# Whole PSUM banks in a kernel's plan, and layer 1's scores tied to layer 0's column products

## Chip, cores and metric

The kernel runs on one core of a Trainium2 chip. The metric is the device time of one launch in microseconds. The kernel before takes 2768.54 us (median of three runs, 2766.03 to 2769.21).

## What is computed

Sixty-four graphs, each with 256 nodes of 256 features (`x`) and a 256 x 256 adjacency (`adj`), go through four layers; each adds to its input and normalizes, all in float32. Cut to what matters (`lrelu` has slope 0.01, `ln` normalizes rows):

```python
# layer 0, 4 heads of 64
X, q, k = heads(lrelu(x @ W_lin + b)), heads(lrelu(x @ W_q)), heads(lrelu(x @ W_k))
adj_h = adj[:, None] * sigmoid(q @ k.T / 8)
deg = sum(adj_h, axis=-1); dis = where(deg > 0, deg ** -0.5, 0)
x = ln(x + ln(dis[..., :, None] * adj_h * dis[..., None, :] @ X) * g + b)
# layer 1, 8 heads of 32
s = where(adj > 0, heads(x @ Wq + bq) @ heads(x @ Wk + bk).T / sqrt(32), NEG)
x = ln(x + softmax(s) @ heads(x @ Wv + bv) @ Wo + bo)
# layer 2
h = (eps * x + adj @ x) @ W1 + b1                      # 1024 wide
x = ln(x + silu(rmsnorm(h) * w) @ W2 + b2)
# layer 3, one head
Wh = x @ W; e = leaky_relu(Wh @ a1 + (Wh @ a2).T, 0.2)
x = ln(x + gelu(ln(softmax(where(adj > 0, e, NEG)) @ Wh) * gamma + beta))
```

## The kernel before

A graph is two blocks of 128 rows by 256 columns, and nearly every operation handles one graph whole: 128 partitions by 2 x 256 numbers. `graph` (L250) lists all operations of one graph; it runs for 64 graphs. It does not issue them. Each call of `op` records the engine, a cost in ns written by hand, the function that issues the instructions, and which `Value`s (tiles) are written and read. `Plan.order` (L98) then puts the some 17,000 operations of all graphs in one order, and `emit` (L737) issues them in that order; each engine works off its own instructions in it, and semaphores are set by the framework from what each tile is written and read by.

The order is that of a list scheduler. It keeps a clock for each engine. Again and again it takes, of all operations whose inputs are planned, the one that can start first, at a tie the one due first. `AHEAD` (L31) limits how early a load may be planned: only when its due turn is at most so many turns away. A turn is a use of one ScalarE table: sigmoid, exp, SiLU and gelu follow each other, four turns to a round, and `ROUND` (L35) says that a graph does layer 0 in its first round, layer 1 two rounds later, layer 2 after five and layer 3 after seven. So in one round some eight graphs at different layers share the engines. `SLOTS` (L37) says how many tiles of each kind there are: the kind "p" is PSUM, eight banks of 512 numbers each in a partition. A tile takes a slot when it is first written and gives it back after its last use.

Most PSUM tiles hold two halves (2 x 256). `Value(..., parts)` lets the plan keep track of parts: a tuple such as `(ps, o)` in the list of writes or reads means this half alone, so that a reader of one half and the writer of the other don't depend on each other in the plan.

TensorE works in three kinds of operation, which the plan calls modes: full (128 x 128 weights; transposes count as a fourth, "transpose"), rows (products with 32 or 64 rows of contraction, placed side by side: L444, layer 0's scores, and L524, layer 1's scores, in two operations of four heads each), and columns (results of 32 or 64 partitions side by side: L462, layer 0's degrees; L484, layer 0's attention times values; L560, layer 1's attention times values). The table `CHANGE` (L23) holds what the plan takes for a change between modes, and `STAY` (L32) a penalty that keeps it from leaving a tiled mode.

Names that come up: L320 is a product of weights with a transposed input, L331 one with the transposed input as weights, L275 a transpose, L591 layer 2's adjacency product, L603 its first and L645 its second dense product, L608 and L610 the two ScalarE reads of L603's result (square, and scale with bias), L622 and L631 the mean of squares and its broadcast with GpSimd's power L626 in between, L635 the multiplication and L637 the SiLU. L407 is the masked softmax's VectorE pass over one half of a bank of scores, L412 its exponential on ScalarE. L660 and L669 belong to layer 3. All DMAs are issued by SyncE (SP), among them the loads (L267) and transposes through device memory (L287 to L306, L547, L549).

Of the kernel before, what the change touches and what calls it, by code (L numbers as in the profile page):

```python
# [19 lines left out]
PE_MM, PE_TR = 432, 109  # L20
# [7 lines left out]
DMA_KB, DMA_SEEN = 4, 1900  # L28

WORDS = {"s": 516, "d": 1024, "b": 2048, "c": 32, "p": 512, "h": 1024}  # L30
AHEAD = 14  # L31
STAY = 200  # L32
NEAR = 1, 1, 3

ROUND = 0, 2, 5, 7  # L35
TAIL = 0, 2, 3, 4
# [42 lines left out]
class Plan:  # L79
# [6 lines left out]
        self.ops, self.turns = [], {}  # L86
        self.graph = 0

    def op(self, engine, cost, fn, w=(), r=(), turn=None, mode="full", after=None, size=0):
        pair = lambda x: x if isinstance(x, tuple) else (x, None)  # L90
        w, r = [pair(x) for x in w], [pair(x) for x in r]
        op = Op(engine, cost, fn, w, r, self.graph, turn, mode, after, size)
        op.table = turn is not None and engine == "ACT"
        if op.table:
            self.turns[turn] = self.turns.get(turn, 0) + 1
        self.ops.append(op)

    def order(self):  # L98
        for i, op in enumerate(self.ops):
            op.index = i  # L100
        for op in reversed(self.ops):
            op.due = min((nxt.due for nxt in op.after), default=4 * (min(op.graph + ROUND[3], self.graphs - 1 + TAIL[3]) + 1))
            if op.turn is not None:
                op.due = min(op.due, op.turn)
        clock = {e: 0.0 for e in AFTER}
        self.free = {k: [(0.0, i) for i in range(n)] for k, n in SLOTS.items()}
        turns, left = sorted(self.turns), dict(self.turns)
        turn, loaded, mode, moved = 0, None, "full", 0.0
        ready = {op for op in self.ops if not op.waits}
        done = []  # L110
        self.busy = {e: 0.0 for e in AFTER}
        while ready:
            best = None
            for op in ready:
                if (op.due - AHEAD if op.first else op.turn or 0) > turns[turn]:
                    continue
                start = clock[op.engine]
                if op.engine == "PE" and mode in ("rows", "columns") and mode != op.mode:
                    start += STAY - 60 * (op.mode == "transpose")
                start = max(start, op.ready)  # L120
                need = {}
                for v in op.values:
                    if v.slot is None:
                        need[v.kind] = need.get(v.kind, 0) + 1
                for kind, n in need.items():
                    free = self.free[kind]
                    if len(free) < n:
                        break
                    start = max(start, sorted(free)[n - 1][0])
                else:  # L130
                    key = start, op.due, op.graph, op.index
                    if best is None or key < best[0]:
                        best = key, start, op
            if best is None:
                raise RuntimeError(f"the plan is stuck at {len(done)} of {len(self.ops)}")
            _, start, op = best
            op.start = start
            ready.discard(op)
            if op.table and op.turn != loaded:
                op.start, loaded = op.start + TABLE_LOAD, op.turn  # L140
            if op.engine == "PE":
                op.start = max(op.start, clock["PE"] + CHANGE.get((mode, op.mode), 0))
                mode = op.mode
            end = clock[op.engine] = op.start + op.cost
            op.landed = end + op.seen
            if op.engine == "SP":
                moved = max(moved, end) + op.size * DMA_KB
                op.landed = max(op.landed, moved + DMA_SEEN)
            self.busy[op.engine] += op.cost
            done.append(op)  # L150
            op.takes = [v for v in op.values if v.slot is None]
            for v in op.takes:
                self.free[v.kind].sort()
                v.slot = self.free[v.kind].pop(0)[1]
            for v in op.values:
                v.uses -= 1
                v.end = max(v.end, op.landed)
                if not v.uses:
                    self.free[v.kind].append((v.end, v.slot))
            for nxt in op.after:  # L160
                nxt.waits -= 1
                nxt.ready = max(nxt.ready, end + ITSELF[op.engine] if nxt.engine == op.engine != "SP" else op.landed)
                if not nxt.waits:
                    ready.add(nxt)
            if op.table:
                left[op.turn] -= 1
                while turn < len(turns) - 1 and not left[turns[turn]]:
                    turn += 1
        assert len(done) == len(self.ops)
        self.span = max(op.start + op.cost for op in done)  # L170
        return sorted(done, key=lambda op: op.start)
# [78 lines left out]
def graph(plan, nc, c, t, out, b):  # L250

    op = plan.op
# [6 lines left out]
    SIG, EXP, SILU, GELU = range(4)  # L259

    def turn(layer, func):
        return 4 * min(b + ROUND[layer], plan.graphs - 1 + TAIL[layer]) + func
# [159 lines left out]
    xT, adjT, x, adj = load("x0T", "xT"), load("adjT", "adjT"), load("x", "x"), load("adj", "adj")  # L422
# [36 lines left out]
    def fn(ps=ps):  # L459
        for i in range(2):  # L460
            for g in range(4):
                pe.matmul(ps.t[g * 32:(g + 1) * 32, i * P:(i + 1) * P], c.ones,  # L462
                          added[i].t.rearrange("p (m g t) -> p m g t", g=4, t=32)[:, :, g], start=True, stop=True)
    op("PE", PE_MM, fn, [ps], added, mode="columns")
    pd = Value("s", "deg")
    op("DVE", 340, lambda ps=ps: dve.transpose(pd.t[:, :N], ps.t[:, :N]), [pd], [ps])
    dp, dis = Value("c", "dp"), Value("c", "dis")
# [11 lines left out]
    def fn(ps=ps):  # L479
        for hp in range(H0 // 2):  # L480
            for m in range(NB):
                for i in range(2):
                    h = 2 * hp + i
                    pe.matmul(two(ps)[i * HD0:(i + 1) * HD0, hp, :], two(v)[:, m, h * HD0:(h + 1) * HD0],  # L484
                              A(h)[:, m, :], start=(m == 0), stop=(m == NB - 1))
    op("PE", 4 * PE_MM, fn, [ps], [v, att], mode="columns")
    y = Value("s", "y", 2)
    if b < NEAR[0]:
        ps = transposed(copy(ps, "yT"))
# [27 lines left out]
    for hq in range(H1 // 4):  # L517
        pss = [Value("p", "ps", 2) for _ in range(4)]

        def fn(hq=hq, pss=pss):  # L520
            for n in range(NB):
                for i in range(4):
                    s = slice(i * HD1, (i + 1) * HD1)
                    pe.matmul(two(pss[i])[:, n, :], two(qT1)[s, hq, n * P:(n + 1) * P], two(kT1)[s, hq, :],  # L524
                              start=True, stop=True)
        op("PE", 2 * PE_MM, fn, pss, [qT1, kT1], turn=turn(1, EXP), mode="rows")
        for pair in range(2):
            e = Value("d", "e", 4)
            for i in range(2):
                softmax(pss[2 * pair + i], negmask, HD1 ** -0.5, e,  # L530
                        lambda n, i=i, e=e: e.t[:, 256 * (2 * i + n):256 * (2 * i + n + 1)],
                        lambda n, i=i: 2 * i + n, r, lambda n, h=4 * hq + 2 * pair + i: 2 * h + n, turn(1, EXP))
            if b < NEAR[1]:
                eT = Value("d", "eT", 2)
                for i in range(2):
                    half = lambda v, i=i: v.t[:, 512 * i:512 * (i + 1)].rearrange("p (n c) -> p n c", n=2)
                    ps = Value("p", "ps", 2)
                    transpose(lambda ps=ps: two(ps), lambda e=e, half=half: half(e), ps, e)
                    op("ACT", 466, lambda ps=ps, eT=eT, half=half: act.copy(half(eT), two(ps)), [(eT, i)], [ps])
                eTs.append((eT, lambda i, m, eT=eT: eT.t.rearrange("p (h m c) -> p h m c", h=2, m=2)[:, i, m]))  # L540
                continue


            eb, far, eT = Value("d", "eb"), Value("h", "far"), Value("d", "eT", 4)
            op("DVE", 1155, lambda e=e, eb=eb: dve.transpose(eb.t.rearrange("p (b g i) -> p g b i", b=4, i=32),  # L545
                                                             e.t.rearrange("p (g b i) -> p g b i", b=4, i=32)), [eb], [e])
            op("SP", 420, lambda eb=eb, far=far: nc.sync.dma_start(far.t, eb.t), [far], [eb], after=3500, size=512)  # L547
            for q in range(4):
                op("SP", 420, lambda far=far, eT=eT, q=q: nc.sync.dma_start(  # L549
                    eT.t[32 * q:32 * q + 32].rearrange("j (a g) -> j a g", a=4),  # L550
                    far.t.rearrange("(a j) (b g) -> b j a g", a=4, b=4)[q]), [(eT, q)], [far], after=4000, size=128)
            eTs.append((eT, lambda i, m, eT=eT: eT.t.rearrange("p (a h n k i) -> p h k n a i", a=4, h=2, n=2, k=2)[:, i, m]))
# [221 lines left out]
```

## Time and profile before

| what | value |
|---|---|
| median of three runs | 2768.54 us |
| the profiled execution's own time | 2761.13 us |
| its span, first to last instruction | 2759.3 us |
| granted TensorE clock | 0.996 |
| TensorE matmuls busy | 2703.5 us, 98% |
| VectorE busy | 2443.0 us, 89% |
| ScalarE busy | 2224.2 us, 81% |
| GpSimd busy | 574.6 us, 21% |
| DMA | 505.17 MB, 183 GB/s on average |

The profile is one execution. Its page gives the busy time of each engine, the span in 40 slices, the DMA queues, the chain that ended last, the costliest groups of instructions by line, and the DMA issues. Behind it stand the trace's views: the busy time in stretches, who waited for whom, and the timeline, in which each row is a run of like instructions with the start, the length, the engine and line, the tiles, and in brackets the idle time before it with what ended it. In the timeline a float32 matmul is two records. A busy TensorE includes modelled ends of matmuls, so that starts are what can be relied on.

### The profile page before, as it was taken

Reading aid. Unit: us, or ns where it says so; the run is one execution under the profiler, and the core shown is the slowest. Engines: PE = TensorE matmul, PEld = TensorE weight load, DVE = VectorE, ACT = ScalarE, POOL = GpSimd, SP = SyncE. Lnnn points to the kernel's source line nnn. Section 1 sums busy time; section 2 is a strip of 40 time slices with the busy share of each in tenths; the row PEclk is TensorE's granted clock in tenths of the full one; section 3 lists DMA queues with packets and bytes.
Section 4 is the critical chain, followed back from the end, with each engine's and each line's share of the span. In section 5 each row is a group of like instructions: output and inputs, shape, how many; then the busy total and the mean of one; then the engine's idle time right before and its main releaser. Section 6 shows DMA issues by size and latency. Waiting matters only on the chain.

```text
span 2759.3 us, 56034 instructions
## 1 busy us (share of the span) xinstructions
PE 2703.5 (98%) x17280; PEld 2160.5 (78%) x17280; DVE 2443.0 (89%) x7426; ACT 2224.2 (81%) x5323; POOL 574.6 (21%) x902
## 2 busy tenths in 40 slices
PE   8999999999999999999999999999999999999997
PEld 6778777777777777787877877788778777777776
DVE  6989998898898889989989989889989899899966
ACT  4878888778788888788878887888888887888775
POOL 1112222122121121221221212212212122122212
PEclk9999999999999999999999999999999999999999
DMA  5677677676677566766756756757667677576651
GB/s 157 199 210 198 172 204 201 176 205 167 193 215 191 157 192 173 211 176 189 210 161 190 217 158 195 211 152 209 184 176 212 166 189 218 143 206 188 184 135 35
DMA packets 710923, 505.17 MB, mean 183 GB/s; under 512 B 310112, under 2 KB 669920, under 8 KB 710624
## 3 DMA queue, kind: packets, MB, share of 16 engines
q1 hardware_dynamic: 710624, 501.59, 65.9%
q8 instruction: 138, 2.26, 0.3%
q14 instruction: 161, 1.32, 0.2%
HBM read 303.44 MB, written 197.92 MB: 182 GB/s over the span
## 4 chain that ended last, share of the span: by engine, by line
PE 75%; DVE 10%; ACT 6%; DMA 4%; SPq 2%; issue 2%; POOL 0%; DVEq 0%; POOLq 0%; ACTq 0%
PE ps L331 13%; PE ps L320 13%; PE ps L645 13%; PE ps L603 11%; PE ps L444 4%; PE ps L524 4%; PE ps L484 3%; PE av L560 3%; PE ps L660 3%; PE ps L591 3%; ACT e L412 2%; DVE e L407 2%; DVE st L345 1%; DMA eT<-far 1%; PE ps L275 1%
## 5 line engine op out<-in xcount | busy, mean ns | idle before, releaser
L412 ACT ACTIVATE e<-e,low 128x256 f32<-128x256 f32 x1152 | 579.8, 505 | 87.5 <-DVE low L407 86.6
L645 PE MATMUL ps<-w,hT 128*128 128x256 f32 x2048 | 478.8, 383 | 5.5 <-ACT hT L637 4.8
L603 PE MATMUL ps<-aggT,w 128*128 128x256 f32 x2048 | 476.4, 382 | 3.8 <-DVE low L407 1.9
L357 POOL TENSOR_SCALAR mv<-mv 128x2 f32<-128x2 f32 x384 | 123.0, 320 | 1573.3 <-DVE mv L347 1012.1
L645 PEld LDWEIGHTS ps<-w,hT 128*128 128x128 f32 x2048 | 382.4, 191 | 68.1 <-issue 6.7
L603 PEld LDWEIGHTS ps<-aggT,w 128*128 128x128 f32 x2048 | 379.7, 190 | 69.4 <-DVE low L407 11.7
L407 DVE CUSTOM_DVE_ANT_0 e<-ps,adj 128x256 f32<-128x256 f32 x1024 | 361.1, 420 | 12.7 <-PE ps L524 11.2
L545 DVE STREAM_TRANSPOSE eb<-e 128x1024 f32<-128x1024 f32 x252 | 306.2, 1224 | 9.3 <-ACT e L412 9.2
L608 ACT ACTIVATE sq<-ps,b 128x256 f32<-128x256 f32 x512 | 242.0, 480 | 82.7 <-PE ps L603 73.0
L358 POOL TENSOR_TENSOR mv<-mv,mhalf 128x2 f32<-128x2 f32 x384 | 298.6, 778 | 32.0
L610 ACT ACTIVATE hT<-ps,br,r 128x256 f32<-128x256 f32 x512 | 288.8, 575 | 10.2 <-PE ps L645 6.7
L372 ACT ACTIVATE x<-y,mv 128x256 f32<-128x256 f32 x384 | 217.3, 602 | 50.9 <-DVE mv L368 48.9
L345 DVE BATCH_NORM_STATS2 st<-y 128x6 f32<-128x256 f32 x640 | 245.2, 413 | 0.9
L412 ACT ACTIVATION_READ_ACCUMULATOR e<-e,low 128x1 f32 x1152 | 225.4, 196 | 0.0
L615 DVE TENSOR_TENSOR sq<-sq 128x512 f32<-128x512 f32 x192 | 131.0, 682 | 98.1 <-ACT sq L608 97.2
L450 DVE TENSOR_TENSOR att<-att,adjT 128x512 f32<-128x512 f32 x256 | 166.6, 681 | 5.1 <-ACT att L448 5.1
L524 PE MATMUL ps<-kT,qT 32*128 32x256 f32 x2048 | 152.0, 400 | 4.3 <-ACT kT L311 4.2
L635 DVE TENSOR_TENSOR hT<-hT,pr 128x1024 f32<-128x1024 f32 x128 | 149.7, 1209 | 5.3 <-PE pr L631 5.3
L470 POOL TENSOR_TENSOR dp<-dp,mhalf 128x8 f32<-128x8 f32 x64 | 106.8, 1668 | 196.3 <-DVE dp L469 166.2
L448 ACT ACTIVATE att<-ps 128x512 f32<-128x512 f32 x256 | 132.2, 603 | 5.6 <-PE ps L444 3.0
L637 ACT ACTIVATE hT<-hT 128x1024 f32<-128x1024 f32 x128 | 128.9, 1050 | 9.1 <-DVE hT L635 7.9
L524 PEld LDWEIGHTS ps<-kT,qT 32*128 32x128 f32 x2048 | 97.9, 184 | 47.5 <-issue 23.3
(113 smaller groups left out, 5486.0 us busy)
## 6 DMA issues: line engine op xcount, KB each, us to landing
far<-eb SPq DMA_DIRECT2D x252, 512.0 KB, 3.8
eT<-far SPq DMA_DIRECT2D x1008, 128.0 KB, 3.9
adj<-in_adj SPq DMA_DIRECT2D x128, 256.0 KB, 4.6
far<-eb SPq DMA_DIRECT2D x488, 64.0 KB, 1.8
x0T<-in_xT SPq DMA_DIRECT2D x64, 256.0 KB, 3.6
adjT<-in_adjT SPq DMA_DIRECT2D x64, 256.0 KB, 4.4
x<-in_x SPq DMA_DIRECT2D x64, 256.0 KB, 4.8
adj<-in_adjT SPq DMA_DIRECT2D x64, 256.0 KB, 5.4
```

Source lines behind the costliest of these rows:

```text
L320: pe.matmul(two(ps)[:, o, :], w.t[:, k, o * P:(o + 1) * P], two(xT)[:, k, :], start=(k == 0), stop=(k == DB - 1))
L331: pe.matmul(two(ps)[:, n, :], two(xT)[:, k, n * P:(n + 1) * P], w()[:, k, :], start=(k == 0), stop=(k == DB - 1))
L345: op("DVE", 328, lambda n=n: dve.bn_stats(st.t[:, 6 * n:6 * n + 6], two(src)[:, n, :]), [(st, n)], [(src, n)])
L358: pool.tensor_tensor(m()[:, :, 2], m()[:, :, 2], c.mhalf[:, :NB], OP.pow)
L407: op("DVE", 345, lambda n=n: dve.tensor_tensor_reduce(out=E(n), in0=two(logits)[:, n, :], in1=two(negmask)[:, n, :], scale=-scale, scalar= ...
L412: op("ACT", 491, lambda n=n: act.activation(E(n), E(n), AF.Exp, bias=low.t[:, n:n + 1], scale=-1.0, accum_out=r.t[:, col(n):col(n) + 1]), ...
L524: pe.matmul(two(pss[i])[:, n, :], two(qT1)[s, hq, n * P:(n + 1) * P], two(kT1)[s, hq, :], start=True, stop=True)
L545: op("DVE", 1155, lambda e=e, eb=eb: dve.transpose(eb.t.rearrange("p (b g i) -> p g b i", b=4, i=32), e.t.rearrange("p (g b i) -> p g b i" ...
L603: pe.matmul(two(ps)[:, i, :], c.w2_1.t[:, k, (j + i) * P:(j + i + 1) * P], two(aggT)[:, k, :], start=(k == 0), stop=(k == DB - 1))
L608: op("ACT", 357, lambda ps=ps, sq=sq, i=i, j=j: act.activation(two(sq)[:, i, :], two(ps)[:, i, :], AF.Square, bias=c.b2_1.t[:, j + i:j + i ...
L610: op("ACT", 491, lambda ps=ps, i=i, j=j: act.activation(Hb(j + i)[:, 0], two(ps)[:, i, :], AF.Identity, bias=c.br2.t[:, j + i:j + i + 1], ...
L645: pe.matmul(two(ps)[:, n, :], Hb(j)[:, 0, n * P:(n + 1) * P], c.w2_2.t[:, j, :], start=(j == 0), stop=(j == HB - 1))
```

## The change

Four things are edited. The line numbers of everything after them move by 46.

- In `op`, a tuple on a PSUM tile loses its part: in the plan every write or read of such a tile is one of the whole bank.
- `AHEAD` goes from 14 to 12.
- `op` takes a `joint`, a pair of a key and a place. `join`, called at the beginning of `order`, makes one operation out of those with the same key: it issues their functions one after the other, has all their inputs and followers, and its cost is the sum with what `CHANGE` says for the modes between. It leaves TensorE in the mode of the last (`leaves`).
- For graphs b from 10 to 55 the degree product of graph b (L462) is joined behind the first four heads' layer 1 scores of graph b - 2 (L524), and the attention times values of graph b (L484) behind the last four heads' scores of graph b - 2.

```diff
-AHEAD = 14
+AHEAD = 12
...
+JOINT = 10, 56
...
-        pair = lambda x: x if isinstance(x, tuple) else (x, None)
+        pair = lambda x: (x[0], None if x[0].kind == "p" else x[1]) if isinstance(x, tuple) else (x, None)
...
+            ops.sort(key=lambda op: op.joint[1])
+            one, fns = ops[0], [op.fn for op in ops]
+            prior = list(dict.fromkeys(p for op in ops for p in before.get(op, ())))
...
+            one.after = list(dict.fromkeys(nxt for op in ops for nxt in op.after))
...
+            one.fn = lambda fns=fns: [fn() for fn in fns]
+            one.cost = sum(op.cost for op in ops) + sum(CHANGE[a.mode, b.mode] for a, b in zip(ops, ops[1:]))
+            one.leaves = ops[-1].mode
...
     def order(self):
         for i, op in enumerate(self.ops):
             op.index = i
+        self.join()
...
-                mode = op.mode
+                mode = op.leaves
...
-    op("PE", PE_MM, fn, [ps], added, mode="columns")
+    op("PE", PE_MM, fn, [ps], added, mode="columns", joint=(("a", b + 0), 1) if JOINT[0] <= b + 0 < JOINT[1] else None)
...
-    op("PE", 4 * PE_MM, fn, [ps], [v, att], mode="columns")
+    op("PE", 4 * PE_MM, fn, [ps], [v, att], mode="columns", joint=(("b", b + 0), 1) if JOINT[0] <= b + 0 < JOINT[1] else None)
...
-        op("PE", 2 * PE_MM, fn, pss, [qT1, kT1], turn=turn(1, EXP), mode="rows")
+        op("PE", 2 * PE_MM, fn, pss, [qT1, kT1], turn=turn(1, EXP), mode="rows", joint=((("a", b + 2), 0) if JOINT[0] <= b + 2 < JOINT[1] else None) if hq == 0 else ((("b", b + 2), 0) if JOINT[0] <= b + 2 < JOINT[1] else None) if hq == 1 else None)
```

No instruction is added or taken away on any engine apart from waits; all that changes is the order in which each engine's queue holds them, and with it the semaphores and the banks and buffers that tiles get.

More of the change, by code (lines that the diff above doesn't have):

```diff
@@ L87, in __init__, with op @@
         self.graph = 0
-    def op(self, engine, cost, fn, w=(), r=(), turn=None, mode="full", after=None, size=0):
-        pair = lambda x: x if isinstance(x, tuple) else (x, None)
+    def op(self, engine, cost, fn, w=(), r=(), turn=None, mode="full", after=None, size=0, joint=None):
+        pair = lambda x: (x[0], None if x[0].kind == "p" else x[1]) if isinstance(x, tuple) else (x, None)
         w, r = [pair(x) for x in w], [pair(x) for x in r]
         op = Op(engine, cost, fn, w, r, self.graph, turn, mode, after, size)
-        op.table = turn is not None and engine == "ACT"
+        op.table, op.joint, op.leaves = turn is not None and engine == "ACT", joint, mode
         if op.table:
@@ L96, in op, with join @@
         self.ops.append(op)
+    def join(self):
+        joints, before = {}, {}
+        for op in self.ops:
+            if op.joint is not None:
+                joints.setdefault(op.joint[0], []).append(op)
+            for nxt in op.after:
+                before.setdefault(nxt, []).append(op)
+        gone = set()
+        for ops in joints.values():
+            if len(ops) == 1:
+                continue
+            ops.sort(key=lambda op: op.joint[1])
+            one, fns = ops[0], [op.fn for op in ops]
+            prior = list(dict.fromkeys(p for op in ops for p in before.get(op, ())))
+            assert not set(prior) & set(ops)
+            for p in prior:
+                p.after = list(dict.fromkeys(one if nxt in ops else nxt for nxt in p.after))
+            one.after = list(dict.fromkeys(nxt for op in ops for nxt in op.after))
+            for nxt in one.after:
+                before[nxt] = list(dict.fromkeys(one if p in ops else p for p in before[nxt]))
+                nxt.waits = len(before[nxt])
+            before[one], one.waits = prior, len(prior)
+            one.fn = lambda fns=fns: [fn() for fn in fns]
+            one.cost = sum(op.cost for op in ops) + sum(CHANGE[a.mode, b.mode] for a, b in zip(ops, ops[1:]))
+            one.leaves = ops[-1].mode
+            one.turn = max((op.turn for op in ops if op.turn is not None), default=None)
+            values = [v for op in ops for v in op.values]
+            one.values = list(dict.fromkeys(values))
+            for v in one.values:
+                v.uses -= values.count(v) - 1
+            gone.update(ops[1:])
+        waits, ops, at = {op: op.waits for op in self.ops}, [op for op in self.ops if not op.waits and op not in gone], 0
+        while at < len(ops):
+            for nxt in ops[at].after:
+                waits[nxt] -= 1
+                if not waits[nxt]:
+                    ops.append(nxt)
+            at += 1
+        assert len(ops) == len(self.ops) - len(gone)
+        self.ops = ops
     def order(self):
```

## The prediction

> **What bounds the kernel now.** I read the page's busy table first, then the stretches of 300 us, the waits of the weight loads, and last the TensorE timeline.
>
> ```profile
> PE 2703.5 (98%) x17280; PEld 2160.5 (78%) x17280; DVE 2443.0 (89%) x7426; ACT 2224.2 (81%) x5323; POOL 574.6 (21%) x902
> 300.00:2600.00 2300.00, 2281.86 (x14622) 1823.86 (x14615) 2084.57 (x6342) 1890.34 (x4515) 492.60 (x771) 1.00 0.68 188
> 2600.00:2760.00 160.00, 134.25 (x728) 110.64 (x728) 110.60 (x342) 109.12 (x255) 28.76 (x53) 0.94 0.39 102
> ```
>
> TensorE is the bound: 98% busy, VectorE 89%, and between 300 and 2600 us nothing else is near full. But the ends of matmuls are modelled, so I don't trust 98%; I use the starts. In this stretch of the timeline the columns are start, length, then the group:
>
> ```profile
> 1403.10 2.00 PE L444 MATMUL ps<-qT,kT 64*128 64x256 f32 x16
> 1405.03 3.72 PE L645 MATMUL ps<-w,hT 128*128 128x256 f32 x16
> 1410.63 1.95 PE L484 MATMUL ps<-att,v 128*64 128x256 f32 x16
> 1412.51 0.70 PE L591 MATMUL ps<-adj,x 128*128 128x256 f32 x2
> 1420.82 1.89 PE L603 MATMUL ps<-aggT,w 128*128 128x256 f32 x8
> 1422.64 1.15 PE L524 MATMUL ps<-kT,qT 32*128 32x256 f32 x16
> 1423.71 0.28 PE L567 MATMUL ps<-ident,r 128*16 128x128 f32 x1
> 1423.83 1.89 PE L603 MATMUL ps<-aggT,w 128*128 128x256 f32 x8
> 1425.65 1.67 PE L524 MATMUL ps<-kT,qT 32*128 32x256 f32 x16
> 1427.25 1.99 PE L603 MATMUL ps<-aggT,w 128*128 128x256 f32 x8
> 1435.73 1.93 PE L560 MATMUL av<-eT,v 128*32 128x256 f32 x32
> 1437.48 0.62 PE L462 MATMUL ps<-added,ones 128*32 128x128 f32 x16
> 1438.03 0.43 PE L631 MATMUL pr<-ident,rs 128*128 128x128 f32 x2
> ```
>
> A full product is two records 0.216 us apart: eight records take 1.73 us (L645: sixteen in 3.45). Before a tiled product the eight of L603 take 1422.64 - 1420.82 = 1.82: entering a tiling costs 0.093 us. L524 does two products' work (0.86) and takes 1423.71 - 1422.64 = 1.07 to its follower; the next L524 takes 1.60, and the extra 0.52 is a wait. L484 takes 1.88 for 1.73, L560 1.75 when L462 follows (1.865 otherwise), L462 0.55 for 0.43.
>
> With these least distances for each pair of neighbours I went through all 17,280 starts: 6.1 us to the first product, 2639.3 us of products and changes of tiling, 95.4 us of waits, 2.0 for the last product and 16.5 us of tail make 2759.3. The waits: 16.4 us before 300 us, 63.6 between 300 and 2600, 15.4 after. So all that can be gained is tiling changes (some 92 us above the pure products of 2547 us, worked out from 0.216 us per record, concurrent tiles once) and 95 us of waits. What is waited for:
>
> ```profile
> PEld ps L603 <- DVE low L407: 11.7, 29, 0.9
> PEld pr L631 <- POOL rs L626: 8.2, 22, 0.8
> PEld ps L524 <- ACT kT L311: 7.7, 9, 1.6
> ```
>
> Short waits, many places: a PSUM bank still being read by the softmax (L407), the power on GpSimd, the copy of kT.
>
> **What the skill says.** "TensorEngine Tiling (Array Packing)", Key Properties: "Mode switching requires drain". The trace agrees, with 0.093 us into a tiling and 0.12 to 0.21 us out. It gives no saving for rows followed by columns, and the trace shows none at the exit: L524 takes 1.075 us before L560 (three times) and 1.076 before a full product. "PSUM — Partial Sum Buffer", PSUM bank collisions: two engines must not be on one bank and quadrant at once, so semaphores have to guard whole banks. The trace agrees with what follows: the second half of a bank is not written until the reader of the first half is done:
>
> ```profile
> 446.34 1.89 PE L320 MATMUL ps<-xT,w_k 128*128 128x256 f32 x8
> 449.90 1.99 PE L603 MATMUL ps<-aggT,w 128*128 128x256 f32 x8 [1.66 <-ACT hT L610]
> ```
>
> Here L603 writes the second half of a bank whose first half L608 and L610 were still reading; the eight of L320 need 1.73 us and 3.56 pass, 1.8 us lost. The old plan, which keeps the halves apart, did not know of this wait.
>
> **The change, part by part.**
>
> *The tie.* Each of 92 column products (46 degree, 46 layer 0 att-value) of graphs 10 to 55 is issued right behind a layer 1 score product of the graph two earlier. I counted neighbours in both built orders. Entries from untiled work into a tiled product fall from 279 to 246, not by 92, because most column products already stood beside another tiled one (L484 before L560 or L462 in 52 of 64 cases, L560 before L462 in 23). Gain: 33 x 0.093 = 3.1 us. L560 directly before L462, which saves 0.115 us, falls from 23 to 6: +2.0. L524 before L524 (0.967 instead of 1.076) falls from 10 to 4: +0.7. L462 before another column product (0.460 instead of 0.550) rises from 2 to 12: -0.9. The sum over all pairs is 2639.3 to 2637.9: **-1.4 us**. The pair L524 then L484 isn't in the trace before; lowest bound, no exit at all (-0.21 us x 47 = -10), highest an added drain of 0.2 us (+9); I take 1.076, as before L560.
>
> The tie makes no new instruction, DMA or table load (ScalarE, VectorE, GpSimd and SP have the same operations: 252 table loads, 3598 DMAs). It adds a wait: a score product also waits for the products of the other graph (L456 added, L476 v), and behind it stands all of TensorE. It needs five free banks of eight together.
>
> *Whole banks in the plan.* In the old order 21 second halves (17 of L603, 4 of L331) stand behind a reader of the first half; in the new order none. The waits there: 1.8 at 449.9, 0.7 at 829.8, 0.5 at 2556, 0.3 at 670, the rest about 0.1 or nothing: some 4 us. Part would show anyway behind another wait, so **-2.5 us** (0 to -4).
>
> *The order that follows.* Everything is planned anew, so the other waits change too. For each place where TensorE waits for another engine I summed the TensorE work, at the distances above, that stands between the last product which the awaited result needs and the waiting product: the cover. In the trace before, cover under 0.9 us: 13 places, 7.9 us of waits; 0.9 to 2: 181 places, 27.7 us (0.153 each); over 2: 1208 places, 54.3 us (0.045 each). The new order has 14, 127 and 1244. L631 behind the power has under 2 us of cover 12 times instead of 33, L524 14 instead of 30, L603 20 instead of 39. At the old rates: +0.6 - 54 x 0.153 + 36 x 0.045 = **-6.1 us**. The rates say little for one place, so I keep -25 to +15.
>
> *The end.* At 2647.8 TensorE runs dry before L645 for 4.8 us and again for 2.9 inside it: sixteen exponentials of the last layer 1 graph stand ahead of the table load and SiLU, while only 5.6 us of products stand between the scores and L645. In the new order 16 L603 (6.9 us) and 4 value products (1.7) stand behind the second score half, and more between the halves. ScalarE must then read some of these between its exponentials (six reads of about 0.5 us), so not all comes back: **-2 us** (-5 to +2).
>
> *AHEAD 14 to 12* and the start. Loads may come half a round later, still some 3 rounds of about 42 us before use; a 256 KB load lands in 3.6 to 5.4 us. On SP the transfers of two yT now stand ahead of w1_v and W1. The L484 products that they carry run at 39 and 47 us, and w1_v is first used at 57.4 us, after the layer 1 scores, which stay ahead of it. Hidden: 0; if not, a microsecond or two at the start.
>
> Sum: -1.4 - 2.5 - 6.1 - 2 = -12 us. The profiled execution took 2761.1 us (span 2759.3, 1.8 outside it), 7.4 below the median of 2768.5. 2761.1 - 12 = 2749.1 there, **2756.5** as a median.
>
> **Rivals.**
> - *The tie costs what it says it saves and the waits merely move* (within 0.2%): only the -1.4 us is sure. For: the old waits repeat where the plan thought there were none, so a new plan may err as much. Time 2767. Chance 0.16.
> - *The new plan, being true to the banks, takes half of the waits between 300 and 2600 away*: -32 us, 2736; its own mean with a part of that 2743. For: the covers of L631, L524 and L603 all rise. Against: three quarters of the old waits stand where cover is over 2 us or rare, from queues on VectorE (89%). Chance 0.20.
> - *Slower: the tied products wait for one another.* Each tie waits for the later of two graphs and for five banks, and all of TensorE waits behind. The price is the wait of an L524 such as that at 1425.65, 0.52 us, at half of the 92 ties: 24 us, less the 12: +12, 2780. It decides from 12 / 92 = 0.13 us per tie. For: banks held by L407 are already the largest named wait, and the first ties have covers of only 0.4 and 0.5 us. Against: over all ties the cover of L484 and L524 rises. Chance 0.18.
> - *As summed*: 2756.5, by itself 2750 to 2763. Chance 0.46.
>
> A difference of 0.2% (5.5 us) is about what can be told from no change. Faster is 0.46 + 0.20 = 0.66, same 0.16, slower 0.18. The range for 8 in 10 leaves out the lower third of the second rival and the upper half of the third: 2738 to 2780.
>
> **What would show it.** In the new profile: entries at 0.093 and L524 before L484 at about 1.08 us (if 0.87, the tie is worth 10 us more); product and tiling time 2637.9; the 21 half-bank waits gone; the wait for L626 below 8.2 us and L603 for L407 below 11.7; the gap near 2650 smaller. I am wrong if waits between 300 and 2600 stay at or over 63 us, or if L524, L462 and L484 now show waits of over 0.13 us at most ties.

## The result and the profile after

The changed kernel takes 2783.66 us (median of four runs, 2780.27 to 2785.83), the kernel before 2767.62 beside it (2766.03 to 2769.21). The ratio is 1.006, with an interval of 1.0044 to 1.0076: slower by 0.6%, where 12 us less were forecast. The profiled execution took 2780.27 us (span 2778.1, granted clock 0.990). All line numbers after the edit are 46 higher: L603, L407, L524 and L687 of before are L649, L453, L570 and L733 here.

First the page's busy table, then the stretches, with the same columns as before.

```profile
PE 2705.6 (97%) x17280; PEld 2171.4 (78%) x17280; DVE 2441.2 (88%) x7426; ACT 2220.9 (80%) x5323; POOL 605.2 (22%) x902
```

```profile
300.00:2600.00 2300.00, 2263.78 (x14506) 1818.39 (x14504) 2063.03 (x6277) 1869.73 (x4491) 510.82 (x758) 0.99 0.68 186
2600.00:2779.00 179.00, 151.09 (x865) 124.24 (x863) 128.79 (x400) 125.58 (x282) 35.96 (x64) 0.96 0.46 119
```

Every engine runs as many instructions as before. In the same 2300 us TensorE starts 14506 matmuls instead of 14622, and VectorE and ScalarE are a little idler too. So the loss is waiting, and it lies in the middle. With the least distances of the prediction the starts give:

| | before | after |
|---|---|---|
| products and changes of tiling | 2639.3 us | 2637.9 us |
| waits before 300 us | 16.4 | 14.4 |
| waits 300 to 2600 us | 63.6 | 87.0 |
| waits after 2600 us | 15.4 | 14.4 |

Next the waits of the weight loads (total, times, longest). The bank read by the softmax, 11.7 us over 29 times before, has become fewer and longer waits; the one for the power has shrunk from 8.2 us.

```profile
PEld ps L649 <- DVE low L453: 16.8, 15, 4.4
...
PEld pr L677 <- POOL rs L672: 2.6, 4, 1.3
...
PEld ps L570 <- ACT kT L357: 2.0, 2, 1.7
```

One of these 4 us waits can be followed to its source. TensorE's timeline:

```profile
1994.20 1.15 PE L570 MATMUL ps<-kT,qT 32*128 32x256 f32 x16
1995.27 0.64 PE L508 MATMUL ps<-added,ones 128*32 128x128 f32 x16
1995.85 0.28 PE L613 MATMUL ps<-ident,r 128*16 128x128 f32 x1
1995.96 1.03 PE L377 MATMUL ps<-w_v,xT 128*128 128x256 f32 x4
2000.96 8.81 PE L649 MATMUL ps<-aggT,w 128*128 128x256 f32 x32 [3.97 <-DVE low L453]
```

L649 needs a PSUM bank that L453 reads. VectorE's timeline shows why L453 is late: it stands in the queue behind a transpose, L333, which waits 4.08 us.

```profile
1994.86 0.13 DVE L724 RECIPROCAL r<-r 128x2 f32<-128x2 f32 x1
1999.08 0.71 DVE L333 STREAM_TRANSPOSE eb<-e 128x512 f32<-128x512 f32 x1 [4.08 <-DMA out<-o]
...
2000.14 0.42 DVE L453 CUSTOM_DVE_ANT_0 e<-ps,adj 128x256 f32<-128x256 f32 x1
```

The transpose writes `eb` and has nothing to do with the result `o`. But in the built program its tile has the SBUF buffer of an `o`, and the store of that `o` was still under way. SyncE's timeline has that store, issued 6.2 us before L333 could start:

```profile
1992.87 0.38 SPq L733 DMA_DIRECT2D out<-o  x1
```

The view of the tile `o` lists everyone who waited for such a store (total us, times), and how long a store took from issue to landing. First the kernel before, then the one after. The waits sum to 10.5 us before and to 39 us after (41.8 by my count of idle VectorE and ScalarE).

```profile
  DVE added L456: 3.8, 1
  ACT kT L311: 3.8, 3
  DVE xb L383: 2.3, 4
  ACT v L311: 0.6, 2
...
DMA to landing us min/median/max: 2.1/3.6/5.7
```

```profile
  DVE eb L333: 12.2, 6
  DVE y L434: 8.8, 2
  DVE added L502: 6.4, 1
  ACT sq L654: 5.6, 2
  DVE xb L429: 3.4, 2
  ACT qT L556: 2.1, 1
...
DMA to landing us min/median/max: 2.1/4.6/6.6
```

The waits return. Around 1324.1, 1493.9, 1662.1, 1830.9 and 2001.0 us, every 169 us or four graphs, TensorE loses 1.2 to 4.1 us, each time behind an L333 that waits for the store of an `o` whose buffer it was given. The Trainium skill, "Perfetto Trace Analysis", Optimization Strategy, says that consistent bubbles, the same gap repeating on the engine that should be saturated, can mean that there isn't enough SBUF or PSUM for the next tile. The trace agrees in form; the experiments test it.

A long wait costs twice. The stretches around 2001 us (granted clock third from the end):

```profile
2001.00:2004.00 3.00, 3.00 (x7) 2.46 (x8) 3.00 (x17) 2.16 (x9) 0.17 (x2) 0.50 0.46 91
2004.00:2007.00 3.00, 3.00 (x14) 2.59 (x14) 3.00 (x11) 2.31 (x8) 2.92 (x3) 0.95 0.50 90
```

In the first 3 us behind the wait the clock is 0.50 and seven matmuls start, in the next 3 us fourteen. Between 300 and 2600 us the kernel after has seven such stretches, 37.5 us in all, the kernel before none. TensorE falls 16.2 us behind its least distances inside them. That is part of the 87.0. It is as much as 16.2 of the 23.4 us by which the middle grew, but it may hold some ordinary waits. Three of the seven stretches (at 465, 513 and 1021 us) stand at a tied pair; what those pairs waited for comes further down.

### The profile page after: what moved, and what is told of

It is laid out like the page before. It is cut to its first block, busy times and chain, and to the rows that moved or that the text cites. A ratio compares the mean times of both kernels' runs of the same rounds, so it can differ in the third digit from the quotient of the medians.

```text
span 2778.1 us, 55957 instructions
## 1 busy us (share of the span) xinstructions
PE 2705.6 (97%) x17280; PEld 2171.4 (78%) x17280; DVE 2441.2 (88%) x7426; ACT 2220.9 (80%) x5323; POOL 605.2 (22%) x902
## 4 chain that ended last, share of the span: by engine, by line
PE 72%; DVE 14%; DMA 6%; ACT 3%; issue 2%; SPq 2%; POOL 1%; DVEq 0%; POOLq 0%; ACTq 0%
PE ps L649 13%; PE ps L366 12%; PE ps L377 12%; PE ps L691 11%; PE ps L530 4%; PE ps L490 3%; PE ps L570 3%; PE av L606 3%; PE ps L706 3%; PE ps L637 3%; DVE e L453 3%; DMA out<-o 2%; DVE eb L591 2%; DMA eT<-far 2%; DVE st L391 2%
## 5 line engine op out<-in xcount | busy, mean ns | idle before, releaser
L649 PE MATMUL ps<-aggT,w 128*128 128x256 f32 x2048 | 472.7, 384 | 16.8 <-DVE low L453 12.0
L403 POOL TENSOR_SCALAR mv<-mv 128x2 f32<-128x2 f32 x384 | 136.0, 354 | 1505.7 <-DVE mv L393 982.7
L649 PEld LDWEIGHTS ps<-aggT,w 128*128 128x128 f32 x2048 | 387.8, 192 | 77.6 <-DVE low L453 16.8
L691 PEld LDWEIGHTS ps<-w,hT 128*128 128x128 f32 x2048 | 383.4, 190 | 62.5 <-issue 6.2
L453 DVE CUSTOM_DVE_ANT_0 e<-ps,adj 128x256 f32<-128x256 f32 x1024 | 361.3, 419 | 26.2 <-PE av L606 15.4
L404 POOL TENSOR_TENSOR mv<-mv,mhalf 128x2 f32<-128x2 f32 x384 | 310.3, 808 | 32.0
L654 ACT ACTIVATE sq<-ps,b 128x256 f32<-128x256 f32 x512 | 244.6, 481 | 70.4 <-PE ps L649 43.7
L418 ACT ACTIVATE x<-y,mv 128x256 f32<-128x256 f32 x384 | 213.3, 610 | 58.9 <-DVE mv L414 55.3
L570 PE MATMUL ps<-kT,qT 32*128 32x256 f32 x2048 | 152.3, 401 | 6.4 <-ACT hT L656 2.6
L494 ACT ACTIVATE att<-ps 128x512 f32<-128x512 f32 x256 | 132.2, 602 | 12.4 <-PE ps L490 11.7
L366 PE MATMUL ps<-x0T,w_q 128*128 128x256 f32 x512 | 131.7, 390 | 5.8 <-DMA x0T<-in_xT 5.8
L570 PEld LDWEIGHTS ps<-kT,qT 32*128 32x128 f32 x2048 | 95.9, 184 | 52.7 <-issue 31.2
## 6 DMA issues: line engine op xcount, KB each, us to landing
eT<-far SPq DMA_DIRECT2D x1008, 128.0 KB, 4.3
```

Source lines behind the costliest of these rows:

```text
L366: pe.matmul(two(ps)[:, o, :], w.t[:, k, o * P:(o + 1) * P], two(xT)[:, k, :], start=(k == 0), stop=(k == DB - 1))
L404: pool.tensor_tensor(m()[:, :, 2], m()[:, :, 2], c.mhalf[:, :NB], OP.pow)
L453: op("DVE", 345, lambda n=n: dve.tensor_tensor_reduce(out=E(n), in0=two(logits)[:, n, :], in1=two(negmask)[:, n, :], scale=-scale, scalar= ...
L649: pe.matmul(two(ps)[:, i, :], c.w2_1.t[:, k, (j + i) * P:(j + i + 1) * P], two(aggT)[:, k, :], start=(k == 0), stop=(k == DB - 1))
L654: op("ACT", 357, lambda ps=ps, sq=sq, i=i, j=j: act.activation(two(sq)[:, i, :], two(ps)[:, i, :], AF.Square, bias=c.b2_1.t[:, j + i:j + i ...
L691: pe.matmul(two(ps)[:, n, :], Hb(j)[:, 0, n * P:(n + 1) * P], c.w2_2.t[:, j, :], start=(j == 0), stop=(j == HB - 1))
```

## The experiments

The plan has 42 slots for the tiles of kind "s" in SBUF, and the pool has 42 buffers. A buffer passes to a later tile after its last use, and the last use of an `o` is its store. **Theory:** the new order hands buffers on too soon after their last use, most harmfully those of `o`. **Rivals:** the tied products wait for one another (the prediction's slower rival); whole banks or AHEAD 12 are at fault; only the store matters and the number of buffers doesn't. All runs compute everything. Each was timed in five rounds against the kernel before, whose medians beside them were 2765.1 to 2766.9 us; an interval belongs to a ratio to it. "Waits" are those of TensorE between 300 and 2600 us.

### The store alone

`o` gets two buffers of its own; the order of instructions is untouched.

```diff
+        pools["o"] = ctx.enter_context(tc.tile_pool(name="pool_o", bufs=2))
...
+        kind = "o" if v.name == "o" else v.kind
+        v.full = pools[kind].tile([P, WORDS[v.kind]], F32, tag=kind, name=v.name)
```

> The changed kernel in its own order, instruction for instruction; only the output tile o gets two buffers of its own (4 KB a partition more), so no other tile takes the buffer of an output store that is still under way. Store theory (VectorE and ScalarE wait some 42 us for such stores in the changed kernel, 10 in the one before, and TensorE starves behind them): 2756 to 2764 us, about 22 less than the changed kernel, and the long TensorE waits at 593, 1196, 1324, 1662 and 2001 us gone. Tie theory (each tied product waits for its second graph and for five banks): 2780 to 2785, waits stay where they are.

Measured: 2742.37 us (0.9911, 0.9895 to 0.9926), 41 less than after, and lower than either theory had it. Waits 50.4 us, none of VectorE or ScalarE for a store of `o`.

> The kernel before in its own order with the same two buffers for o. Store theory: it had 10 us of such waits, a part of them ahead of TensorE (1.4 us at 1758): 2759 to 2766 us, 2 to 8 us less than before. Tie theory: says nothing, 2767.

Measured: 2764.89 us (0.9991, 0.9984 to 0.9999), waits 64.6. The same edit is worth next to nothing in the old order. So what the store's buffer costs belongs to the new order. Since two buffers were also added, this doesn't yet tell the store from the number.

### The parts of the change, in the common pool

No ties: `JOINT = 64, 64`. The tie alone: halves kept apart in the plan (the old `pair`) and `AHEAD = 14`.

```diff
-JOINT = 10, 56
+JOINT = 64, 64
```

> The changed kernel without the tie (whole banks in the plan and AHEAD 12 stay), planned anew. Tie theory: the loss goes, 2760 to 2768 us. Store theory: the order is another one, so which tile meets a store is another throw; by TensorE products and tilings alone 1 us more than the changed kernel; 2760 to 2785, and the time follows the store waits.

Measured: 2751.1 us (0.9938, 0.9921 to 0.9954), waits 58.0, idle time behind stores 21.4 us in 10 places (after: 41.8 in 19).

```diff
-AHEAD = 12
+AHEAD = 14
...
-        pair = lambda x: (x[0], None if x[0].kind == "p" else x[1]) if isinstance(x, tuple) else (x, None)
+        pair = lambda x: x if isinstance(x, tuple) else (x, None)
```

> The kernel before with the tie alone (halves of banks kept in the plan, AHEAD 14). Tie theory: all of the loss, 2780 to 2790 us. Store theory: another throw, 2760 to 2785; products and tilings alone give 2.5 us less than before.

Measured: 2842.8 us (1.0274, 1.0256 to 1.0292), waits 128.0, behind stores 45.0 us. Neither theory allowed for these two times: the first lies below both ranges, the second above both. With 42 buffers the tie is what turned a gain of 16 us into a loss of 16. Whether by its own waits or by what it does to the buffers is left to the next runs.

### All parts, with the store's own buffers

With the three switches (halves or whole banks, tie or none, AHEAD 14 or 12) there are eight orders. Six more runs fill the table; each has the edit of the first diff, and of the later diffs what its name in the table says.

> Whole banks and AHEAD 12 without the tie, and o in two buffers of its own; the order is that of the run without the tie. That run held 21 us of VectorE and ScalarE waits for stores. Store theory: 2730 to 2738 us, some 17 less. If the tie itself loses time (after it is freed of stores it takes 2742): below 2742 is a tie that costs; 2742 or more is a tie that pays its 1 us of tilings.

> The tie alone on the plan before (halves of banks, AHEAD 14), o in buffers of its own. Its waits for stores were 45 us. Store theory for that part: 2800 to 2810 us. What stays above 2767 is then not stores; if tie and halves of banks don't go together, the tie with whole banks and AHEAD 14 lies far lower.

> The changed kernel with AHEAD 14 (tie and whole banks stay), o in buffers of its own. If AHEAD matters little by itself: 2737 to 2752 us. If loads one half round earlier do the harm seen with the tie alone: near 2800.

> The kernel before with whole banks in the plan alone (no tie, AHEAD 14), o in buffers of its own. If whole banks are what makes the order better: 2735 to 2755 us, where the kernel before with the same buffers takes 2765. If AHEAD 12 does it: about 2765.

> The changed kernel with halves of banks kept in the plan (tie and AHEAD 12 stay), o in two buffers of its own. With AHEAD 14 the tie takes 2803 with halves and 2795 with whole banks. If AHEAD 12 is what lets the tie go through: 2742 to 2760 us. If it takes both whole banks and AHEAD 12: near 2790.

> The kernel before with AHEAD 12 alone, o in two buffers of its own. The kernel before with those buffers takes 2765, whole banks alone 2758, whole banks with AHEAD 12 2745. If the two add: about 2752 us. If AHEAD 12 needs whole banks: 2760 to 2770.

Measured, in us, with the waits in brackets:

| plan | no tie, AHEAD 14 | no tie, AHEAD 12 | tie, AHEAD 14 | tie, AHEAD 12 |
|---|---|---|---|---|
| halves | 2764.9 (64.6), before_own_store | 2786.2 (74.0), ahead_only_own_store | 2802.6 (94.6), tie_only_own_store | 2757.7 (62.5), parts_kept_own_store |
| whole banks | 2757.6 (55.3), banks_only_own_store | 2745.4 (51.0), no_tie_own_store | 2794.9 (90.1), ahead14_own_store | 2742.4 (50.4), after_own_store |

The ratios: 0.992 (0.9907 to 0.9933) for no_tie_own_store, 1.0133 (1.0115 to 1.015) tie_only_own_store, 1.0109 (1.0093 to 1.0124) ahead14_own_store, 0.997 (0.9958 to 0.9982) banks_only_own_store, 0.9972 (0.9962 to 0.9983) parts_kept_own_store, 1.0082 (1.0068 to 1.0096) ahead_only_own_store.

Three things follow. With whole banks every column is faster, by 7, 41, 8 and 15 us (at the 8 the intervals of the two runs overlap); that rival falls. The tie costs 37 to 38 us at AHEAD 14 with either plan of the banks. At AHEAD 12 it gains 28 us with halves and 3 with whole banks, where the intervals overlap. So its price isn't a wait that each tie has. And AHEAD, costed at nothing, decides between 2795 and 2742 us for the tied order; 12 is the better value in three of four cases, and it isn't what made the change slow. The number of "s" tiles alive at once, averaged over the planned time, goes with most of the table (not with ahead_only_own_store, 21 us slower than before_own_store, where both theories had it faster or the same): 33.2 for no tie and AHEAD 12, 34.65 for after, 36.65 for tie and AHEAD 14 (before: 35.25). At 40 or more of 42 the tied order with AHEAD 14 stands for 19% of the time, after for 2%. So the store of `o` isn't all: with no wait for it, tie_only_own_store still waits 94.6 us.

### The number of buffers

The same order, the common pool, two buffers more; the plan goes on counting 42.

```diff
-bufs=SLOTS[kind]
+bufs=SLOTS[kind] + 2 * (kind == "s")
```

> The changed kernel's own order; the common pool holds 44 buffers instead of 42, and o stays in it, so a stored buffer is still handed on while its store is under way. If the store's landing is what hurts: the freed buffer is handed out about as soon, most of the waits stay, 2765 to 2783 us. If it is scarcity of buffers, and o's own buffers only helped as two more: 2740 to 2750.

Measured: 2733.26 us (0.9889, 0.9875 to 0.9902), 50 less than after, 9 less than with the two buffers given to `o`, and lower than the theory of short buffers had it. The stretch, the wait for L453's bank and those who waited for `o`:

```profile
300.00:2600.00 2300.00, 2286.20 (x14790) 1842.84 (x14789) 2102.87 (x6403) 1908.40 (x4582) 520.41 (x774) 1.00 0.70 191
```

```profile
PEld ps L649 <- DVE low L453: 4.7, 15, 0.6
```

```profile
  ACT v L357: 0.9, 2
  DVE y L541: 0.5, 1
```

In 2300 us TensorE now starts 284 more matmuls than in after. The same 15 places wait for L453, but 0.6 us at most instead of 4.4. Waits in the middle are 43.9 us.

Then the reverse: `o` has its own two buffers, and the common pool only 40, 42 in all.

```diff
+bufs=SLOTS[kind] - 2 * (kind == "s")
```

> The changed kernel's own order; o in two buffers of its own, the common pool cut to 40, so that the memory is the same as in the changed kernel. If the store's landing is what hurts: 2740 to 2755 us. If scarcity of buffers: 2780 or more.

Measured: 2803.4 us (1.014, 1.0126 to 1.0153), 20 more than after, waits 107.8. No one waits for a store of `o`. The store of layer 1's small transpose (`rT`, L616) has taken its place. The view of that tile counts those who waited for the store and, with a few us, for the copy L615 before it:

```profile
  ACT sq L654: 9.2, 5
  DVE added L502: 5.9, 2
  ACT e L719: 5.4, 2
...
DMA to landing us min/median/max: 1.3/2.4/7.4
```

So "only the store matters" falls. The number of buffers counts, and a store is merely a last user that takes long.

To see that in the order itself I took the built programs and counted, for each "s" buffer, the TensorE work between its last use and its next tile. Reuse within 3 us, and the times that the previous owner was an `o` stored less than 6 us before:

| kernel | within 3 us | after a young store | time |
|---|---|---|---|
| before | 296 | 21 | 2767.6 |
| after | 296 | 49 | 2783.7 |
| no_tie | 174 | 21 | 2751.1 |
| tie_only | 836 | 49 | 2842.8 |
| after_s44 | 101 | 25 | 2733.3 |
| after_own_s40 | 726 | 2 | 2803.4 |
| ahead14_own_store | 681 | 2 | 2794.9 |
| ahead_only_own_store | 128 | 2 | 2786.2 |

Before and after differ in the second count alone. The table goes with the times except in its last row, which stays unexplained: that order keeps 17 second halves behind a reader of the first (before: 21), and I didn't find what it waits for. Runs that the table leaves out loosen it further. By a recount, which gives 324 for after, there are some 250 for after_own_store (2742.4 us), 360 for parts_kept_own_store (2757.7) and 75 for before_s44 (2757.1). Within one order fewer such reuses went with less time in all four orders that ran with more than one set of buffers; between orders the count decides little.

Why does a buffer come so soon, when the plan's clock holds a store's landing too? It reckons 3.4 to 12.3 us from issue to landing in after, where the trace shows 2.1 to 6.6. The built program doesn't use the plan's slots: `emit` asks the pool for any tile of the kind, and the pool mostly gives the buffer whose last use was issued longest ago. In after only 1087 of 2704 tiles follow the tile that the plan had put before them. 71 start, by the plan's own clock, before the buffer they got is free, 35 of them behind an `o` (before: 55 and 14); in the plan's slots none does. For all five L333 of the 169 us series the plan had a slot that was free 2.4 us earlier, and the program took the buffer of an `o` that by the same clock was free 5.4 us later. So the buffers were short for the way they are handed out, not in the plan. Two more put off each reuse; whether the plan's own slots would do as well with 42 was not run.

### Both orders with buffers enough

> The kernel before in its own order with 44 common buffers. Reuse theory (a tile that gets a buffer soon after its last user, above all a transfer that has not landed, makes VectorE and ScalarE wait and TensorE behind them; two more buffers took 50 us off the changed kernel): the kernel before gets little, 2745 to 2760 us, and the changed kernel with 44 (2733) is then ahead of it by some 12 to 25, which is what the order is worth when buffers are not short. If the order is worth nothing: 2733 too.

Measured: 2757.14 us (0.9971, 0.9963 to 0.998), waits 63.4.

> Whole banks and AHEAD 12 without the tie, in its own order with 44 common buffers. In its built order 47 buffers are handed on within 3 us of TensorE work of their last use, 54 to 66 in comparable ones and 296 in the changed kernel. Reuse theory: 2728 to 2738 us. If then below the changed kernel with 44 (2733), the tie costs even so; if above, it pays.

Measured: 2737.17 us (0.9901, 0.9888 to 0.9914), waits 49.6.

> The tie alone (AHEAD 14, halves of banks), in its own order with 44 common buffers. With 42 it takes 2843 us and hands on 836 buffers within 3 us of their last use; with 44 it is 305, as many as the changed kernel has with 42 (296, 2784 us). Reuse theory: 2765 to 2790 us. If the tie itself costs the time: above 2800.

Measured: 2784.02 us (1.0067, 1.0055 to 1.008), waits 86.8; 59 us less than tie_only. It is still 27 us slower than before_s44, so for this order two buffers take away most of the loss and not all; whether the rest is reuse (305 such reuses are left) or the tie's own waits isn't told apart.

> The changed kernel in its own order with 45 common buffers, as many as fit. 54 instead of 101 buffers are handed on within 3 us of their last use. Reuse theory with what is left of such waits (4 us of stores in the run with 44): 2728 to 2734 us. If 44 are enough: 2733.

Three buffers more (`3 * (kind == "s")`). Measured: 2730.8 us (0.9879, 0.9866 to 0.9892), waits 40.4; the lowest of all, 1.2% faster than before. From 44 to 45 the intervals overlap.

At 44 buffers the changed order is 24 us faster than the old one (2733.3 against 2757.1), at 42 it is 16 us slower. With the ties it takes 4 us less than without (2733.3 against 2737.2), but these intervals overlap: the tie no longer costs, and that it pays isn't shown. Added waits inside a tied pair, from the start of its score product to the start of the column product: 13.1 us at 7 of the 93 seams in after, 7.5 at 4 in after_own_store, 2.5 at 3 in after_s44, 0.8 in after_s45. They do exist in after, as at 511 us:

```profile
509.16 0.47 ACT L654 ACTIVATE sq<-ps,b 128x256 f32<-128x256 f32 x1 [5.00 <-PE ps L637]
511.45 0.69 PE L570 MATMUL ps<-kT,qT 32*128 32x256 f32 x2 [1.70 <-ACT hT L656]
512.43 1.80 PE L570 MATMUL ps<-kT,qT 32*128 32x256 f32 x10 [0.28 <-DVE y L434]
```

The pair waits for banks that ScalarE and VectorE have not emptied. ScalarE is late because L654 waited 5.00 us for the product L637. `sq` takes nothing from that product; in the built program it has the buffer of the adjacency that L637 read last. So this is the same cause, with a product as the last user instead of a store. With two more SBUF buffers and the same ties most of it is gone.

## Why the prediction was wrong, step by step

- *Tilings, -1.4 us.* Right: 2639.3 became 2637.9. The pair that the trace didn't show, L524 before L484, takes 1.075 to 1.076 us in 46 of 47 cases, the value taken; the other, at 688 us, takes 1.70 and holds a wait.
- *Half-bank waits, -2.5 us.* The sign is right. The 21 orderings are gone, and with own stores whole banks gain 7 to 41 us; how much of that is the waits themselves and how much the new order isn't told apart.
- *"The order that follows", -6.1 us.* Here the prediction failed. (The terms shown give -6.0, and the "three quarters" of old waits in the second rival are some seven tenths; neither matters.) Waits in the middle went from 63.6 to 87.0 us, which is +23.4 instead of -6.1. The cover is TensorE work between a product and the need for its result. It says whether the readers have time, if they start when they can. They didn't: VectorE and ScalarE stood at the heads of their queues for a buffer, and the banks behind them stayed full. The term "time from a buffer's last use to its next tile", with a store's landing of 2.1 to 6.6 us in it, was put at nothing, as if the program used the plan's slots. With 44 buffers in both orders the middle falls from 63.4 to 43.9, -19.5 us, where covers and half banks together had -8.6. So the sign was right once the buffers allowed it, and the size too small; that it is the covers that brought it isn't shown.
- *"Hidden: 0" for AHEAD.* The start took no harm (16.4 to 14.4 us), but that was the wrong question. AHEAD also sets how many tiles are alive, and it is worth from -52 to +21 us in the table.
- *The end, -2 us.* -1.0 (15.4 to 14.4). The prediction misread the 2.9 us inside L645 as TensorE running dry again: the trace has the half clock there (line below), and most of its records start 0.43 us apart instead of 0.216.
- *Size of a long wait.* It was costed at its own length. The half clock behind it adds to that; up to 16.2 us of the loss is there. The trace of before had one case, the 4.8 us wait at 2647.8.
- *The signs.* The wait for the power fell to 2.6 us as said. That of L603 for L407 rose to 16.8, and the middle is over 63 us, the mark of being wrong. The slower rival came near the time (2780) by luck, with another mechanism: 7 of 93 pairs waited, not half, and two buffers take most of that away.

```profile
2651.00:2655.00 4.00, 2.24 (x5) 1.85 (x6) 4.00 (x7) 3.97 (x6) 1.10 (x3) 0.57 0.54 174
```

## What to carry to other kernels

A change of order changes how soon each buffer is used again; before trusting a new order, count for every pool the time from a buffer's last use to its next tile, and let a store's last use be its landing, not its issue. Count it in the built program: the buffers that the pool gives needn't be the slots that the plan reckoned with. When the same gap returns at a fixed distance, add a buffer or two without touching the order: such a run shows how much of the loss lies in the buffers. Only then judge the order, since a good one may look bad (here +16 us with 42 buffers, -24 with 44).

## What the hardware showed beside

- The granted clock halved for 3.4 to 6.8 us behind some waits of TensorE. The Trainium skill, "TensorE: Matmul & The Clock Gate", Why this matters for your kernels, advises against idle gaps of over some 3 us between bursts of matmuls. The trace agrees roughly: the waits of 4.1 us at 2001.0 and at 1196.4 were followed by the half clock, but so were those of 2.8 at 1324.1 and 2.3 at 1662.1, and those of 3.1 at 593.0 and 3.0 at 633.7 were not. No sharp threshold can be read from this.
- The same 64 stores of `o` land in 3.6 us (median) in the kernel before and in 4.6 after, still 4.6 in after_own_store and 4.4 in after_s44. So the longer landing goes with the order and not with the waits; what else is in the DMA queues at that time was not examined.
